# First and last rounds of an attention stage: values, adapter and feed-forward weights moved between rounds

## The chip, the cores and the metric

One Trainium2 chip, one of its cores. The metric is the device time of one execution of the whole program in microseconds (us), lower is better. Each kernel is run several times and the median counts.

## What is computed

The input is x of shape (4, 256, 512), that is four batches of 256 tokens with 512 channels. Three residual layers follow, with a feed-forward layer twice:

```python
x = x + attn_a(layernorm(x))     # causal attention, 32 heads of 16, rotary, plus an adapter of 10 tokens
x = x + ffn(layernorm(x))        # 512 -> 512, rows and columns chosen by 64 centroids
x = x + attn_b(layernorm(x))     # Mamba2 mixer: 128 heads of 64, 8 groups, state 128
x = x + ffn(layernorm(x))        # the same weights again

# attn_a
q, k, v = split(x @ w_attn.T); q, k = rope(q), rope(k)
y  = softmax(mask(q @ k.T / sqrt(16))) @ v
ak, av = adapter_wte @ w_attn.T
y += gating * softmax(q @ ak.T / sqrt(512)) @ av
out = y @ w_proj.T

# ffn
dots = softmax(x @ centroids.T / 0.1); hits = dots > 0.01
dense = x @ weight.T + bias
out = where(any(hits, 1)[:, None] & any(hits, 0)[assignments][None, :], dense, 0)
```

The column choice `any(hits, 0)` needs the hits of all 1024 tokens. So the first feed-forward layer can compute its dense part tile by tile, but it takes its results into x only when all eight tiles of 128 tokens are through.

## The kernel before

All of x lies in the on-chip memory as eight tiles of 128 tokens. A matrix product in 32-bit precision is made as three products of high and low parts (`mm3`, lines 107 to 114: L112 is high by high, L113 and L114 the two cross terms); `split` (L102 to L105) makes the parts, with a copy on ScalarE (ACT, L104) and a subtraction on VectorE (DVE) or on GpSimd (POOL) (L105).

`attention` (L232 on) works in 32 **rounds**: round i takes batch b = i // 8 and a step u = i % 8 of four heads. Round i computes the `scores` of its four heads on TensorE (PE, L441 and L448), their maxima on DVE (L453) and their exponentials on ACT (L456, eight activations, each with a read of the accumulator). Later rounds go on with it: round i + 1 turns the exponentials (`turn`, L471, PE transposes into the PSUM tile `ptr`, then copies, L472), round i + 2 weighs the values with them (`weigh`, L481 and L487), round i + 3 gathers the result into `y` (`gathered`, L498, L504).

Beside this main line, generators carry work that a round takes along. A generator yields a stage ("long", "values" or "turn") and the round from which it may go on; `step(stage, i)` moves those that are due. In before, `moved` treats round 0 as "the next round" (`v[1] if v[1] else i + 1`). The generators are:

- `prepared(b)`: norm of the batch's two token tiles (`normed`, transposes L163), queries, keys (`made`, 12 matmuls of 128x512 each, then the rotation on DVE L280 to L284 and POOL L286) and values (12 matmuls a tile, then an ACT copy, L383). For batch 0 it runs whole ahead of the rounds; for batches 1 to 3 it runs during the batch before.
- `pieces(b, q, f)`: builds the queries (f = 0) and keys (f = 1) of eight heads: `stacked` (ACT L304, POOL L305), then PE transposes into `trp` (L393) and copies L395, which are on DVE for f = 0 and on ACT for f = 1.
- `adapter`, `adapter_scores`, `adapted`: the ten adapter tokens.
- `closed(b, ks)`: the finished `y` is turned (L555) and projected (L566, 24 matmuls of 128x512 for a batch, tile `po`), then `finished` adds it to x (L582), and for batches 2 and 3 makes the statistics (L135, L136) and the root (L140, a square root on ACT, which needs another activation table than the exponential) of the feed-forward norm.
- `fed(f, t)`: one tile of the feed-forward layer: `normed` in the stage "turn", and `Feed.tile` in the stage "long" of the round after (24 matmuls of 128x288, tile `pd`, L112 to L114; then ten DVE instructions and one exponential, L205 to L218).

TensorE follows the order in which the program is written (`manual_schedule`). For the other engines and the DMA queue a planner fixes the order when the program is built: of what it takes to be ready it picks the earliest in program order.

The weights of the output projection (`wp`) are loaded and split ahead of the rounds, on ACT and POOL (`weights(wp_s, wproj, "pc1", nc.gpsimd)`, L629). The weights of the feed-forward layer (`fw`) are loaded and split when `Feed` is made, in round 24 (L679 to L689, L188 to L191), on ACT and DVE. Its eight tiles start ("turn") in the rounds `FEEDS = (25, 26, 27, 29, 31, 32)` and, for tiles 6 and 7, after the last projection; the 32nd and later "rounds" hold no scores any more and are called the tail here. After the tail `select` (L222) counts the hits and the mixer follows. It is the far longer part of the program.

The PSUM tiles are in rings: `m` with three buffers (`trp`, `ptr`, `pq`, `pd`, `po`, `tr` and others share them), `sc` with four for the scores, `py` with one.

Of the kernel before, what the change touches and what calls it, by code (L numbers as in the profile page):

```python
# [77 lines left out]
def hybrid_kernel(  # L78
# [93 lines left out]
    class Feed:  # L172


        def __init__(self, name, w1, p2):
# [12 lines left out]
            for k in range(KC):  # L188
                r = p2.tile([P, 2, FH], F32, name=f"{name}r", tag="fr")
                load(r, ffw[:, k])  # L190
                split([v[:, k] for v in self.w], r)  # L191
            self.new = t("x", [P, TT, C])
            self.hits = t("h", [P, NCL])
            nc.gpsimd.memset(self.hits, 0.0)

# [36 lines left out]
    def attention(later):  # L232
        with ExitStack() as es:
# [19 lines left out]
            def weights(w, src, tag, engine):  # L253
                for k in range(0, KC, 2):
                    r = p2.tile([P, 2, C], F32, name="ar", tag=tag)
                    load(r, src[:, k : k + 2, :])
                    for j in range(2):
                        split([v[:, k + j, :] for v in w], r[:, j, :], engine)
# [100 lines left out]
            def prepared(b):  # L359

                where = (ps, "m") if b else (ps_s, "sc")
                r = 8 * (b - 1)
# [17 lines left out]
                made(1, 1)  # L380
                for c in range(2):
                    yield "long", r + 5 + c
                    nc.scalar.copy(vs[b % 2][:, c, :C], projected(xs[c], wv_s, where))  # L383
# [160 lines left out]
            def closed(b, ks):  # L544
# [5 lines left out]
                yield "turn", 0  # L550
# [6 lines left out]
                if 3 not in ks:  # L557
                    return
                st = state.pop(b)
                pos = []  # L560
                for c in range(2):
                    if c == 0 or b < B - 1:
                        yield "long", 8 * b + {B - 1: 0, B - 2: 12}.get(b, 14) + c
                    pos.append(ps.tile([P, C], F32, name="po", tag="m"))
                    cs = slice(c * P, (c + 1) * P)
                    mm3(pos[c], [[v[:, k, cs] for v in st["yT"]] for k in range(KC)],  # L566
                        [[v[:, k, :] for v in wp_s] for k in range(KC)])
                    if b < B - 1:
                        finished(b, c, pos[c])
                if b < B - 1:  # L570
                    return
                for c, po in enumerate(pos):
                    finished(b, c, po)
                for t, xn in late.items():
                    tr = ps.tile([P, KC, P], F32, name="tr", tag="m")
                    xs = [p2.tile([P, KC, P], F32R, name=f"axs{j}", tag=f"axs{j}") for j in range(2)]
                    feed.norm.turn(xn, tr, xs)
                    late[t] = xs

            def finished(b, c, po):  # L580
# [4 lines left out]
                if feed is None:  # L585
                    return
                feed.norm.stats(t)
                feed.norm.root(t, t + 1)
                if b < B - 1:
                    slow.append(fed(feed, t))  # L590
                else:
                    late[t] = p2.tile([P, C], F32, name="axn", tag="t1")
                    feed.norm.scale(t, late[t])

            def fed(f, t):
                yield "turn", 0
                xs = normed(f.norm, t)
                yield "long", 0
# [25 lines left out]
            for _ in prepared(0):  # L624
                pass
            for t in range(2, TT):
                norm.stats(t)
            norm.root(2, TT)
            weights(wp_s, wproj, "pc1", nc.gpsimd)  # L629
            jobs, slow = [], []  # L630

            def adapter():
                split(wt, wte_s)
                yield "long", 0
                ak = adapter_weights()
                yield "turn", 0
# [8 lines left out]
            feed, late = None, {}  # L645
            asides, nexts = [], {}
            FEEDS = (25, 26, 27, 29, 31, 32)

            def moved(j, i):
# [4 lines left out]
                else:  # L654
                    nexts[j] = v[0], v[1] if v[1] else i + 1
# [5 lines left out]

            begin(0)
# [6 lines left out]
            with tc.manual_schedule(engines={nc.tensor.engine}):  # L669
                for i in range(n + 6):  # L670
                    b, u = divmod(i, 8)
                    if i < n:
                        if u == 0:
                            if i:
                                begin(b)
                            if b + 1 < B:
                                moved(prepared(b + 1), i)
                        es_[i] = scores(b, u)
                    if i == n - 8:  # L679
# [6 lines left out]
                        for t in range(4):  # L686
                            feed.norm.stats(t)
                        feed.norm.root(0, 4)
                        slow += [fed(feed, t) for t in range(4)]  # L689
                    if i in FEEDS:  # L690
                        moved(slow.pop(0), i - 1)
                    step("long", i)
                    if part:
                        next(part)
                    part = None
                    if i < n and u % 2 == 0 and i > 0:
                        asides.append(adapter_scores(b, u // 2))
                        next(asides[-1])
                    step("values", i)
                    if 2 <= i <= n + 1:  # L700
                        yss[i - 2] = weigh(*divmod(i - 2, 8), eTs.pop(i - 2))
                    if 1 <= i <= n:
                        eTs[i - 1] = turn(es_.pop(i - 1))
                    if 3 <= i < n + 3:
                        gathered(*divmod(i - 3, 8), yss.pop(i - 3))
                    while asides:
# [566 lines left out]
```

## Time and profile before

| what | value |
|---|---|
| median of 3 runs | 1900.88 us (1900.85 to 1903.54) |
| profiled execution, its own time | 1898.88 us |
| span of the profiled execution | 1897.1 us |
| mean granted TensorE clock | 0.988 |
| PE busy | 1813.4 us (96%) |
| DVE, ACT, POOL busy | 1474.0, 1381.5, 370.0 us |
| first scores of round 0 | 36.39 us |
| first scores of round 31 | 331.45 us |
| `select` after the first feed-forward layer (L222) | 376.60 us |

The span is the time from the first to the last instruction; the execution's own time has 1.8 us more around it, and lies 2.0 us under the median. "Busy" is the time in which an engine had an instruction running; a PE that is busy isn't one at its peak. A line of the timeline gives the start, the duration, the engine, the line of the kernel, the operation with its tiles (out<-in), the shapes and the number of merged instructions, and in brackets how long the engine had been idle before and what ended that. The view by stretches gives the busy time of each engine, the number of instructions in brackets, then the granted clock (1.00 is full), the share of DMA and GB/s.

### The profile page before, as it was taken

The numbers are of one execution on the slowest core, as the hardware profiler recorded it, in microseconds if no ns is written. First come the engines' busy times: TensorE is split into PE (matmuls) and PEld (weight loads), VectorE is DVE, ScalarE is ACT, GpSimd is POOL, SyncE is SP. The second block draws the span as 40 slices with busy tenths as digits, with TensorE's granted clock in tenths as the row PEclk, the third lists the DMA queues.
The fourth block names the chain that finished last, engine by engine and source line by source line (L and its number), as shares of the span: only waits on it lengthen the run. The fifth ranks groups of instructions, "written<-read, shape, count | busy, mean of one in ns | idle before, by whom it ended". The sixth has DMA issues, their size and how long they took to land.

```text
span 1897.1 us, 29902 instructions
## 1 busy us (share of the span) xinstructions
PE 1813.4 (96%) x10690; PEld 1450.5 (76%) x10690; DVE 1474.0 (78%) x2324; ACT 1381.5 (73%) x2875; POOL 370.0 (20%) x308
## 2 busy tenths in 40 slices
PE   7889989789999999999999999999999999999997
PEld 6667767676777887878788778777787888787786
DVE  6566667688998778777877787778778877877777
ACT  5667677368898768777877787678777876786753
POOL 5212110011311211211212121212221221122100
PEclk8999999999999999999999999999999999999999
DMA  4000000125555454554545464545554545455341
GB/s 142 1 1 1 22 15 1 32 62 172 176 188 180 147 170 150 160 157 150 170 150 158 145 184 144 176 143 167 149 171 143 158 156 164 148 162 166 112 124 49
DMA packets 151909, 240.35 MB, mean 127 GB/s; under 512 B 12368, under 2 KB 77520, under 8 KB 151760
## 3 DMA queue, kind: packets, MB, share of 16 engines
q1 hardware_dynamic: 151760, 238.44, 40.1%
q8 instruction: 84, 1.38, 0.3%
q14 instruction: 65, 0.53, 0.1%
HBM read 202.75 MB, written 35.65 MB: 126 GB/s over the span
## 4 chain that ended last, share of the span: by engine, by line
PE 75%; DVE 9%; ACT 9%; DMA 3%; issue 3%; POOL 1%; SPq 0%; DVEq 0%; ACTq 0%; POOLq 0%
PE pp L112 12%; PE pp L113 11%; PE pp L114 11%; PE pyy L991 8%; PE pog L112 6%; PE pog L114 6%; PE pog L113 6%; PE trx L976 3%; ACT e L456 3%; PE ptr L471 2%; DMA wor<-in_wout_dram 2%; DVE acc L917 1%; PE pd L114 1%; ACT L921 1%; DVE eT L472 1%
## 5 line engine op out<-in xcount | busy, mean ns | idle before, releaser
L112 PE MATMUL pp<-mx,w 128*128 128x512 f32 (+1 forms) x1160 | 465.5, 401 | 8.1 <-DVE acc L917 7.6
L114 PE MATMUL pp<-mx,w 128*128 128x512 f32 (+1 forms) x1160 | 454.3, 392 | 0.0
L113 PE MATMUL pp<-mx,w 128*128 128x512 f32 (+1 forms) x1160 | 454.2, 392 | 0.0
L917 DVE SCALAR_TENSOR_TENSOR acc<-pp,cw_s,acc 128x1012 f32<-128x1012 f32 (+2 forms) x240 | 304.9, 1270 | 23.0 <-ACT acc L910 22.4
L965 DVE TENSOR_TENSOR em<-em,gm 128x1536 f32<-128x1536 f32 x128 | 228.0, 1781 | 94.2 <-ACT em L959 85.9
L112 PEld LDWEIGHTS pp<-mx,w 128*128 128x128 f32 x1160 | 218.5, 188 | 65.7 <-issue 10.4
L953 POOL TENSOR_SCALAR_AFFINE_SELECT r<-r 128x512 f32<-128x512 f32 x128 | 153.0, 1196 | 526.7 <-DMA r<-cumd 433.8
L114 PEld LDWEIGHTS pp<-mx,w 128*128 128x128 f32 x1160 | 218.6, 188 | 45.3 <-issue 0.4
L113 PEld LDWEIGHTS pp<-mx,w 128*128 128x128 f32 x1160 | 218.8, 189 | 40.6 <-issue 0.7
L1014 POOL TENSOR_TENSOR sq<-sq,acc 128x1024 f32<-128x1024 f32 x55 | 132.7, 2412 | 574.3 <-ACT acc L1013 574.3
L104 ACT CAST w<-wr 128x512 fp32r<-128x512 f32 x144 | 88.4, 615 | 189.1 <-PE pp L113 158.3
L112 PE MATMUL pog<-wo,gh 128*128 128x512 f32 x512 | 204.6, 400 | 0.0
L114 PE MATMUL pog<-wo,gh 128*128 128x512 f32 x512 | 200.4, 392 | 0.0
L113 PE MATMUL pog<-wo,gh 128*128 128x512 f32 x512 | 200.0, 391 | 0.0
L958 ACT ACTIVATE em<-r,col_t 128x128 f32<-128x128 f32 x512 | 164.9, 390 | 48.2 <-PE pyy L991 46.5
L991 PE MATMUL pyy<-em,xd 128*64 128x256 f32 (+1 forms) x2048 | 189.1, 330 | 2.6 <-DVE em L965 2.6
L991 PEld LDWEIGHTS pyy<-em,xd 128*64 128x64 f32 x2048 | 134.1, 137 | 63.8 <-issue 21.7
L961 ACT ACTIVATE em<-r,col_t 128x128 f32<-128x128 f32 x512 | 166.5, 388 | 0.0
L949 DVE TENSOR_SCALAR em<-r,col_t 128x128 f32<-128x128 f32 x512 | 136.0, 325 | 12.2 <-PE pyy L991 10.1
L977 DVE TENSOR_TENSOR xd<-trx,dt_t 128x512 f32<-128x512 f32 x128 | 86.2, 683 | 56.1 <-PE trx L976 56.0
L105 DVE TENSOR_TENSOR w<-wr,w 128x512 fp32r<-128x512 f32 x139 | 98.3, 708 | 37.2 <-ACT w L104 36.8
L456 ACT ACTIVATE e<-sc,nmx 128x256 f32<-128x256 f32 (+1 forms) x256 | 103.4, 430 | 30.4 <-DVE nmx L453 30.4
(287 smaller groups left out, 3176.4 us busy)
## 6 DMA issues: line engine op xcount, KB each, us to landing
wr<-in_win_dram SPq DMA_DIRECT2D x287, 256.0 KB, 2.8
r<-cumd SPq DMA_DIRECT2D x128, 512.0 KB, 4.2
spill<-gb SPq DMA_DIRECT2D x63, 512.0 KB, 2.8
gr<-spill SPq DMA_DIRECT2D x120, 256.0 KB, 3.4
wor<-in_wout_dram SPq DMA_DIRECT2D x64, 256.0 KB, 3.1
out_dram<-x SPq DMA_DIRECT2D x8, 256.0 KB, 2.3
x<-in_x_dram SPq DMA_DIRECT2D x1, 1536.0 KB, 10.0
gr<-spill SPq DMA_DIRECT2D x8, 192.0 KB, 2.7
```

Source lines behind the costliest of these rows:

```text
L112: nc.tensor.matmul(o, lh, rh, start=(first and k == 0), stop=False)
L113: nc.tensor.matmul(o, lh, rl, start=False, stop=False)
L114: nc.tensor.matmul(o, ll, rh, start=False, stop=(last and k == n - 1))
L456: nc.scalar.activation(es_[c][:, 2 * j + pr, :], sc[:, j, :], AF.Exp, bias=nm[:, j : j + 1], accum_out=rs[:, c, h : h + 1],)
L917: nc.vector.scalar_tensor_tensor(av[:, :, d:], pv[:, :, : L - d], cw_s[:, ch, tap : tap + 1], av[:, :, d:], ALU.mult, ALU.add,)
L949: nc.vector.tensor_scalar(e[:, b, 2, :], rv[:, b, 1, :], col_t[:, h, b, 1:2], 0.0, ALU.subtract, ALU.min,)
L953: nc.gpsimd.affine_select(rv[:, :, 0, :], rv[:, :, 0, :], pattern=[[0, B], [1, P]], compare_op=ALU.is_ge, fill=-1e30, base=0, channel_mult ...
L958: nc.scalar.activation(e[:, b, 1, :], rv[:, b, 1, :], AF.Exp, bias=col_t[:, h, b, 2:3])
L961: nc.scalar.activation(e[:, b, 0, :], rv[:, b, 0, :], AF.Exp, bias=col_t[:, h, b, 0:1])
L965: nc.vector.tensor_tensor(e, e, gm, ALU.mult)
L991: nc.tensor.matmul(py[d, b, k * P :], xd[:, 2 * b + k, d], es2[hh][:, b, 2 * k : 2 if k == 0 else 3, :].rearrange("p s i -> p (s i)"), sta ...
L1014: (nc.gpsimd if n < NB - 1 else nc.vector).tensor_tensor(sq, sq, x2, ALU.add)
```

## The change

It reorders the attention stage; no arithmetic is changed.

1. **Values in the rounds.** `prepared(0)` no longer runs whole ahead of the rounds. Its norms, queries and keys do; its values (2 x 12 matmuls) come in the stage "long" of rounds 0 and 1, into PSUM ring `m` in place of `sc`. Round 0 is now a round of its own right, so `prepared(1)`, which had started in round 1, starts in round 0 and goes one round earlier throughout (norm in rounds 0 and 1, queries and keys in 1 to 4, values in 5 and 6).
2. **Projection weights.** `wp` is loaded in round 3, into a staging buffer that shares its place (`ya`) with the adapter's tokens and its products, and is split there.
3. **Feed-forward weights.** `Feed` is made at the end of round 23; a quarter of its weights is loaded and split at the end of each of the rounds 23 to 26, the subtraction on POOL in place of DVE. The statistics of the first four tiles go along, one a round, and their root follows at the end of round 26 (before: round 24).
4. **Feed-forward tiles.** Tiles 0 and 1 are turned in rounds 28 and 29 and multiplied in rounds 29 and 30; tile 2 is turned in round 31. Tiles 2 to 5 are multiplied in the tail, tiles 6 and 7 at its end as before. Before, tiles 0 to 3 were multiplied in rounds 26, 27, 28 and 30.
5. **Tail.** It is written out instead of running as rounds 32 to 37. Tile 4 is multiplied after the last `gathered`, the projection of batch 3 follows, and then tile 5, while the norms of tiles 6 and 7 are made.
6. **Roots.** Batch 2's two tiles share one root in place of one each.
7. The second feed-forward layer (`Feed("g")`) calls its weights in a loop of its own, on DVE as before.

```diff
-            for k in range(KC):
-                r = p2.tile([P, 2, FH], F32, name=f"{name}r", tag="fr")
-                load(r, ffw[:, k])
-                split([v[:, k] for v in self.w], r)
...
+        def weights(self, k, engine=nc.vector):
+            r = self.p2.tile([P, 2, FH], F32, name=f"{self.name}r", tag="fr")
+            load(r, ffw[:, k])
+            split([v[:, k] for v in self.w], r, engine)
...
-                r = 8 * (b - 1)
+                r = 8 * (b - 1) if b else -5
...
+                where = (ps, "m")
                 for c in range(2):
                     yield "long", r + 5 + c
                     nc.scalar.copy(vs[b % 2][:, c, :C], projected(xs[c], wv_s, where))
...
                 feed.norm.stats(t)
-                feed.norm.root(t, t + 1)
+                if b == B - 1 or c == 1:
+                    feed.norm.root(t if b == B - 1 else t - 1, t + 1)
...
-            weights(wp_s, wproj, "pc1", nc.gpsimd)
...
-            FEEDS = (25, 26, 27, 29, 31, 32)
+            FEEDS = {28: 0, 29: 1, 31: 2}
...
-                    nexts[j] = v[0], v[1] if v[1] else i + 1
+                    nexts[j] = v[0], i + 1 if v[1] is None else v[1]
...
+            first = prepared(0)
+            moved(first, -9)
+            while nexts[first][1] < 0:
+                moved(first, -9)
...
+                    if i in FEEDS:
+                        moved(fed(feed, FEEDS[i]), i - 1)
+                    if i == 3:
+                        weights(wp_s, wproj, "ya", nc.gpsimd, p1)
...
+                    if i in range(23, 27):
+                        feed.weights(i - 23, nc.gpsimd)
+                        feed.norm.stats(i - 23)
+                    if i == 26:
                         feed.norm.root(0, 4)
...
+                b = B - 1
+                step("long", n)
+                yss[n - 2] = weigh(b, 6, eTs.pop(n - 2))
+                eTs[n - 1] = turn(es_.pop(n - 1))
+                gathered(b, 5, yss.pop(n - 3))
+                step("turn", n)
+                moved(fed(feed, 3), n - 1)
+                step("turn", n)
+                step("long", n + 1)
+                step("values", n + 1)
+                yss[n - 1] = weigh(b, 7, eTs.pop(n - 1))
+                gathered(b, 6, yss.pop(n - 2))
+                moved(closed(b, (0, 1, 2)), n)
+                moved(fed(feed, 4), n)
+                step("turn", n + 1)
+                gathered(b, 7, yss.pop(n - 1))
+                moved(closed(b, (3,)), n)
+                step("long", n + 2)
+                moved(fed(feed, 5), n)
+                step("turn", n + 2)
+                pos = [projected_out(b, c) for c in range(2)]
+                late = {}
+                for c, po in enumerate(pos):
+                    t = 2 * b + c
+                    finished(b, c, po)
+                    late[t] = p2.tile([P, C], F32, name="axn", tag="t1")
+                    feed.norm.scale(t, late[t])
+                step("long", n + 3)
+                for t, xn in late.items():
+                    tr = ps.tile([P, KC, P], F32, name="tr", tag="m")
+                    xs = [p2.tile([P, KC, P], F32R, name=f"axs{j}", tag=f"axs{j}") for j in range(2)]
+                    feed.norm.turn(xn, tr, xs)
+                    late[t] = xs
+                for t, xs in late.items():
+                    feed.tile(t, xs, [ps_s.tile([P, FH], F32, name="pd", tag="sc") for _ in range(2)])
```

## Prediction

> **What bounds the kernel now.** I read the page first, then the chain of waits in order of time, then stretches cut at the first score matmul (L441) of each round, then PE's timeline. The change touches only the first 376.6 us; the mixer behind it keeps its instructions. The page's chain says what sets the pace over the whole span:
>
> ```profile
> PE 75%; DVE 9%; ACT 9%; DMA 3%; issue 3%; POOL 1%; SPq 0%; DVEq 0%; ACTq 0%; POOLq 0%
> ```
>
> That is an average, and ahead of round 0 it is wrong. There the chain runs through POOL:
>
> ```profile
> 25.71 1.25 POOL r L286
> ...
> 28.01 0.69 POOL wp L105
> ...
> 29.28 1.30 POOL wp L105
> 30.58 1.24 POOL r L286
> 31.82 1.92 POOL wp L105 x2
> ...
> 34.67 0.46 POOL st L305
> ...
> 36.39 1.12 PE sc L441 x8
> ```
>
> The last rotation (r, L286) and the last stack of keys (st, L305) queue behind the projection weights (wp), which nobody needs before round 14. In round 1, PE then waits for the adapter's keys:
>
> ```profile
> 49.56 1.03 PE L335 MATMUL tra<-con,st 20*128 20x20 f32 x8 [2.56 <-POOL st L305]
> ```
>
> Rounds 24 to 29 as stretches, and two pieces of the chain in rounds 24 and 25:
>
> ```profile
> 259.31:269.94 10.63, 7.72 (x66) 5.97 (x66) 8.79 (x20) 8.54 (x28) 3.85 (x5) 0.84 0.00 0
> 269.94:280.32 10.38, 7.59 (x71) 6.18 (x70) 4.07 (x9) 9.04 (x28) 0.87 (x2) 0.92 0.01 2
> 280.32:292.30 11.98, 10.98 (x91) 8.91 (x90) 10.06 (x28) 7.43 (x28) 0.92 (x2) 0.93 0.00 1
> 292.30:301.90 9.60, 8.96 (x81) 7.44 (x80) 6.98 (x19) 6.96 (x26) 1.08 (x2) 1.00 0.01 2
> 301.90:314.28 12.38, 11.65 (x94) 9.69 (x94) 10.29 (x27) 8.55 (x26) 0.00 (x0) 1.00 0.00 1
> 314.28:322.28 8.00, 7.84 (x67) 6.15 (x67) 5.29 (x12) 6.55 (x23) 0.00 (x0) 1.00 0.00 1
> ```
>
> ```profile
> 259.87 2.44 DVE fw L105 x2
> ...
> 272.09 1.28 ACT L456
> ```
>
> Rounds 24 and 25 have little for PE (7.7 and 7.6 us busy) and still take over 10 us. In 24, two feed-forward splits stand before the maxima on DVE; in 25 the exponentials wait for their table after the root. The tail lasts 45.15 us (331.45 to 376.60) with PE busy for 35.59; its worst place and its last two stretches:
>
> ```profile
> 339.59 0.40 PE L112 MATMUL pd<-fw,axs 128*128 128x288 f32 x1 [2.87 <-ACT axs L104]
> 340.72 0.44 PE L112 MATMUL pd<-fw,axs 128*128 128x288 f32 x1
> 356.38:366.82 10.44, 8.38 (x45) 6.07 (x41) 6.96 (x18) 3.93 (x8) 0.00 (x0) 1.00 0.00 0
> 366.82:376.60 9.78, 7.26 (x52) 6.87 (x52) 7.27 (x23) 4.87 (x10) 1.26 (x1) 1.00 0.01 2
> ```
>
> A tile multiplied right after its own turning makes PE wait 2.87 us, and the clock drops: its matmuls then follow each other at 0.24 us instead of 0.13.
>
> **Part by part, in us against the profiled span of 1897.1.**
>
> *First scores.* Without wp, the last rotation starts when DVE's L284 ends (28.63) and not at 30.58; the ACT copy (0.41) and the POOL part (0.46) follow at once, where st now waits from 32.3 to 34.67. So st ends at 31.0 instead of 35.13; transposes and copy (1.26 as now) bring the scores to 32.1: −4.3. The values leaving PE alone would bring little, as PE sat idle for 3.14 before the last trp. If DVE also puts the statistics of tiles 2 to 7 later, −5.2; if the planner fills POOL with something else, 0. I take −4.3, the reading of the chain itself.
>
> *Rounds 0 to 2.* Round 0 gets 12 value matmuls (12 x 0.233 = 2.8) and the transposes of a norm (0.6): +3.4, as it has only 0.67 of PE idle. Round 1 gets 12 values and the first 12 query matmuls of batch 1, 5.6; of these the wait of 2.56 and part of another 1.07 are cover: +2.2. Round 2 swaps queries for keys, loses a norm's transposes (0.6) and should start on a full clock (it ran half its time at the half clock, mean 0.88, because of round 1's idle): −2.0. Sum +3.6. Round 7 loses 12 matmuls and the wait on their copy (PE idle 1.69 before ptr, ended by ACT av L383): 8.95 falls to about 7.0, since a round with keys on ACT needs its exponentials, two copies and the turn, some 7 (round 3 takes 7.71): −1.9. So this part is +1.7; from +5.6 (nothing covered: 24 matmuls) to −2.1 (all 7.7 of PE idle in rounds 0, 1, 2 and 7 filled).
>
> *Projection weights in round 3.* Two loads on an idle DMA queue, four ACT copies (4 x 0.58), four POOL subtractions (4 x 1.28). Needed from round 14; ACT is busy 6.00 of 7.71 in round 3 and 5.45 of 9.60 in round 4. Behind POOL's four stand a rotation and stacks used a round later. If the shared buffer comes free only with batch 0's adapter products, the loads go to rounds 10 to 12 and still make round 14. Cost 0.4, from 0 to 2.3 (all four copies on the path).
>
> *Rounds 23 to 31.* Splits: one ACT copy (0.68) and one POOL subtraction a round, 1.28 x 576/512 = 1.44, where POOL is busy for 8.0 of 80.57. Round 24 then looks like round 16 (8.25, the same work without feed-forward): −2.4. Round 25 loses the table load and a tile's transposes: −2.3. Round 26 loses 24 pd matmuls (24 x 0.133 = 3.2) and transposes (0.6), and starts warm: −4.5. Round 27 loses the same 3.8 but receives the root with its two table loads (2 x 1.28 + 0.30), and exponentials and copies hold it at 7 anyway: −0.4. Round 28 loses 3.2 of pd, gains 0.6 of transposes: −2.8. Round 29 gains a tile, as PE is busy 7.84 of 8.00: +3.3. Rounds 30 and 31 keep theirs. Sum −9.1; from −5 (only the two stalls go) to −11. The merged root takes two loads (2 x 1.28) off ACT in round 28, but PE is idle there for only 0.7 and not because of them: 0.
>
> Here a page speaks for more. The Trainium skill, "ScalarE: Activation LUTs", section "What ACT_TABLE_LOAD costs", gives 2.66 us a switch with the drain, so the merged root would bring an estimated 5.3 and the forecast would fall by that. Another speaks against the change: "GPSIMD Engine Reference", section "Engine selection", says to keep elementwise work of two inputs on VectorE because GpSimd takes twice as long; were these four splits on the path, they would cost an estimated 3 instead of gaining. This case's rows decide both by who waits: nobody waits for POOL's fw, and DVE's 2.44 stand on the chain.
>
> *Tail.* Tiles 2 and 3 now stand where 4 and 5 stood, to 356.4, with the same waits. Then come tiles 4 and 5 as additions: 2 x (3.2 + 0.6) = 7.6. They cover a wait of 1.02 before the last try and most of one of 0.73 before tile 6; tile 4's own wait for its split costs about 0.7 and DVE's order about 0.3. DVE was busy some 15 of the last 20 and gets 2 x 4.0 (norm 0.55, split 0.69, ten small ones 2.8): 23 in 27. Tail +6.8; from +5.5 (waits filled) to +17.6 (below).
>
> *Sum:* −4.3 + 1.7 + 0.4 − 9.1 + 6.8 = −4.5. The span becomes 1892.6, the execution 1894.4 (1.8 more), and against the median 1900.9 − 4.5 = **1896.4 us**.
>
> **The rivals.**
>
> *A, slower: tiles 4 and 5 each pay the price of 339.59.* Place: after tile 4's transposes only one short gather stands before its matmuls. If ACT's copy queues behind the copies of yT, and DVE's part behind the adds of y, PE waits 2.87 and the clock drops, so that a tile costs 2.87 + 5.3 + 0.6 = 8.8: two are +17.6 where I have 6.8 after cover, net −4.3 + 1.7 + 0.4 − 9.1 + 17.6 = +6.3, or 1907.2. Against it: tile 5 has the 24 projection matmuls (5.6) between turn and use. It decides from about 1 us of wait before pd of both tiles.
>
> *B, no change: the first rounds give back what the preamble gains.* The scores come 4.3 earlier, but the 24 matmuls and the batch-1 work are covered by nothing: +5.6 in place of +1.7; and wp costs 1. Net about 0: −4.3 + 5.6 + 1.0 − 9.1 + 6.8 = 0.0, 1900.9. For it: PE idles longer ahead of round 0 and may start it cold (round 0 ran at 0.73 already).
>
> *C, the change does less than it says:* rounds 24 to 28 shorten only by their stalls (−5), because exponentials and the ring of three m buffers hold a round near 8: −0.4, 1900.5. Against it: round 21, with keys on ACT and 12 matmuls, takes 7.39.
>
> **How the numbers follow.** My case 0.60, A 0.17, B 0.12, C 0.11. A measurement of this kernel can tell about 0.2%, 3.8 us. Of my case some 0.50 lie beyond −3.8, 0.10 inside; A gives 0.16 slower and 0.01 same; B and C give 0.16 same, 0.03 faster, 0.04 slower. Together faster 0.53, same 0.27, slower 0.20. Low end: first scores −5.2, early rounds 0, rounds 23 to 31 −11, tail +5.5, wp 0, in sum −10.7: 1890. High end: A at 1907.
>
> **What would show it.** Right: first L441 near 32; no wp on POOL ahead of it; rounds 0 to 2 together near 35 (31.5 now); round 24 near 8.2 and round 26 near 7.5; no fw on DVE; first L441 of round 31 at 317 to 322; from there to L222 near 52. Wrong: a first L441 later than 34; rounds 24 to 28 in sum over 48 (55.0 now); PE waits over 2 us with the clock at 0.5 before pd of tiles 4 and 5; `select` after 377 by the trace's clock.

## The result, and the profile after

The changed kernel is slower by a third of a percent: 1907.19 us in the median of 7 runs (1905.57 to 1909.53) against 1900.85 us of 7 runs of the kernel before, a ratio of 1.0035, 95% interval 1.0023 to 1.0046. The forecast was 1896.4 us. The profiled execution took 1905.57 us, with a span of 1903.8 us (1.8 us lie around it, as before). In the traces the difference goes like this, in us against the kernel before (lengths are taken between the first score matmuls of the rounds; L441 is now L443, `select` is L223):

| stretch | predicted | trace of after |
|---|---|---|
| up to the first scores | −4.3 | −3.2 (36.39 to 33.20) |
| rounds 0 to 2 | +3.6 | +7.9 (31.5 to 39.4) |
| rounds 3 to 8, with wp | −1.5 | −0.65 |
| rounds 9 to 22 | 0 | −0.5 |
| rounds 23 to 30 | −9.1 | −10.1 |
| round 31 to `select` | +6.8 | +10.7 (45.15 to 55.82) |
| behind `select` | 0 | +2.5 |
| sum | −4.5 | +6.7 |

In rounds 9 to 22 the programs differ in one thing that the list of the change leaves out: the adapter's scores of the even rounds now come ahead of the stage "long". Every kernel below has this order too, and the −0.5 most likely comes from it (x8, otherwise as before up to round 22, has it as well, next to two halved clocks).

The page's chain hardly changed in its shares (PE 73% in place of 75%, ACT 12% in place of 9%), and tells nothing of this. The chain in order of time does, over the same stretch that was shown of before:

```profile
29.07 0.46 POOL st L306
29.53 1.23 POOL r L287
...
33.20 1.11 PE sc L443 x7
...
35.28 0.43 PE pq L112
...
39.45 0.23 PE pq L113
...
50.08 0.54 ACT wp L104
50.69 1.69 POOL wp L105 x2
...
53.17 1.27 POOL r L287
...
54.89 0.43 PE tra L336 x4
```

Three things are to be seen. No wp stands ahead of the last rotation any more (29.53, 30.58 before); a stack of the next pieces (29.07) has taken a little of its place. The values (pq L112 from 35.28) are now on the chain itself, at 0.43 us each, where the same kind of matmul takes 0.23 four us later. And wp is not in round 3: the planner found its loads and splits ready and drew them into rounds 0 and 1, where they and the rotation of batch 1 (53.17) stand ahead of the adapter's keys, which PE waits for at 54.89 (49.56 before).

PE's timeline shows where the clock went, with the idle time in brackets:

```profile
27.18 0.87 PE L395 MATMUL trp<-con,st 128*128 128x128 f32 x8 [1.78 <-POOL st L306]
31.77 0.75 PE L395 MATMUL trp<-con,st 128*128 128x128 f32 x4 [3.73 <-POOL st L306]
```

With the values ahead of round 0 and no wp (x3 below), PE has one wait of 1.50 us in this place. The stretches (rounds 0, 1 and 2; then round 24; then round 31 to `select`; start and end, length, busy time of PE, PE's weight loads, DVE, ACT and POOL, then PE's clock):

```profile
33.20:44.04 10.84, 10.71 (x49) 8.06 (x49) 4.50 (x11) 7.19 (x24) 2.31 (x4) 0.72 0.15 49
44.04:58.46 14.42, 11.89 (x78) 9.61 (x78) 6.31 (x13) 9.73 (x34) 8.37 (x11) 0.92 0.13 37
58.46:72.60 14.14, 13.59 (x85) 10.35 (x84) 7.62 (x14) 6.32 (x24) 2.23 (x4) 0.84 0.00 0
...
263.05:273.17 10.12, 7.59 (x65) 6.06 (x64) 8.12 (x18) 9.52 (x29) 4.08 (x5) 0.83 0.00 0
...
324.92:380.74 55.82, 44.85 (x318) 38.24 (x317) 35.39 (x102) 23.28 (x58) 3.94 (x5) 0.94 0.06 19
```

Round 0 is full of PE (10.71 of 10.84) at a clock of 0.72. Round 26 is as short as hoped (7.83 us), with rounds 25, 27 and 28 (7.70, 6.25 and 9.57 us); round 24 is not, and the end is 4 us longer than expected. On the chain, round 24 waits for the root of tiles 0 to 3 and its two table loads, which the program has at the end of round 26:

```profile
264.78 1.28 ACT L140
266.08 0.30 ACT frs L140
266.39 1.28 ACT L458
```

Places of PE and ScalarE's activation tables in the end (332.95 is tile 2, 352.67 tile 4, 370.11 the turning of tile 7, 371.59 tile 6):

```profile
332.95 0.61 PE L112 MATMUL pd<-fw,axs 128*128 128x288 f32 x1 [2.81 <-ACT axs L104]
...
352.67 0.40 PE L112 MATMUL pd<-fw,axs 128*128 128x288 f32 x1 [0.51 <-ACT axs L104]
...
370.11 0.97 PE L163 MATMUL tr<-con,axn 128*128 128x128 f32 x4 [3.14 <-DVE axn L155]
...
371.59 0.44 PE L112 MATMUL pd<-fw,axs 128*128 128x288 f32 x1
```

```profile
358.00 1.28 ACT L140 ACT_TABLE_LOAD   x1
...
365.96 1.28 ACT L209 ACT_TABLE_LOAD   x1 [3.41 <-DVE fnm L207]
...
367.68 1.28 ACT L140 ACT_TABLE_LOAD   x1
```

The exponential of tile 5 was set between the roots of tiles 6 and 7, so ACT changes its table twice more, the scaling of tile 7 comes late, PE idles 3.14 us and multiplies tile 6 at half the clock. Tiles 4 and 5 themselves waited 0.51 us and not at all.

### The profile page after: what moved, and what is told of

Same layout as the page of the kernel before. It is cut to its first block, busy times and chain, and to the rows that moved or that the text cites. A ratio compares the mean times of both kernels' runs of the same rounds, so it can differ in the third digit from the quotient of the medians.

```text
span 1903.8 us, 29900 instructions
## 1 busy us (share of the span) xinstructions
PE 1815.8 (95%) x10690; PEld 1453.8 (76%) x10690; DVE 1473.3 (77%) x2319; ACT 1379.9 (72%) x2874; POOL 346.9 (18%) x312
## 4 chain that ended last, share of the span: by engine, by line
PE 73%; ACT 12%; DVE 8%; DMA 3%; issue 3%; POOL 1%; SPq 0%; ACTq 0%; DVEq 0%; POOLq 0%
PE pp L112 12%; PE pp L113 11%; PE pp L114 11%; PE pyy L1016 8%; PE pog L112 6%; PE pog L114 6%; PE pog L113 6%; ACT e L458 4%; PE trx L1001 3%; DMA wor<-in_wout_dram 1%; PE ptr L473 1%; DVE acc L942 1%; ACT L946 1%; PE pg L956 1%; ACT acc L946 1%
## 5 line engine op out<-in xcount | busy, mean ns | idle before, releaser
L112 PE MATMUL pp<-mx,w 128*128 128x512 f32 (+1 forms) x1160 | 465.1, 401 | 9.1 <-DVE acc L942 8.6
L112 PEld LDWEIGHTS pp<-mx,w 128*128 128x128 f32 x1160 | 218.2, 188 | 66.9 <-issue 11.0
L978 POOL TENSOR_SCALAR_AFFINE_SELECT r<-r 128x512 f32<-128x512 f32 x128 | 125.1, 977 | 548.9 <-DMA r<-cumd 484.6
L112 PE MATMUL pog<-wo,gh 128*128 128x512 f32 x512 | 204.4, 399 | 0.0
L974 DVE TENSOR_SCALAR em<-r,col_t 128x128 f32<-128x128 f32 x512 | 137.7, 328 | 12.6 <-PE pyy L1016 10.1
```

The source lines that it names most:

```text
L112: nc.tensor.matmul(o, lh, rh, start=(first and k == 0), stop=False)
L974: nc.vector.tensor_scalar(e[:, b, 2, :], rv[:, b, 1, :], col_t[:, h, b, 1:2], 0.0, ALU.subtract, ALU.min,)
L978: nc.gpsimd.affine_select(rv[:, :, 0, :], rv[:, :, 0, :], pattern=[[0, B], [1, P]], compare_op=ALU.is_ge, fill=-1e30, base=0, channel_mult ...
```

## Experiments

Theory: the loss is made in the first rounds (values without cover, on a halved clock) and at the end (the tables' order), while the rounds between do what they should. Rivals: wp's new place, the earlier start of batch 1, or the late part as a whole is the cause. Every kernel x1 to x14 was timed together with the kernel before (13 to 34 runs of it each time, medians 1901.5 to 1902.6). The third column is the start of round 9, the fourth of `select`, both from one trace each. Kernels that differ from each other only behind round 22 (x5, x7, x9, x10, x11) lie up to 3.0 us apart at round 9, so a single trace tells less than the ratios do. Ratios of kernels that were timed together (x1 to x4, x5 to x8, x9 to x12, x13 and x14) compare best.

| kernel | ratio (95%) | round 9 | `select` |
|---|---|---|---|
| before | 1 | 118.63 | 376.60 |
| after | 1.0035 (1.0023 to 1.0046) | 122.72 | 380.74 |
| x1 root first | 1.0014 (1.0006 to 1.0023) | 122.32 | 379.05 |
| x2 first part undone | 0.9994 (0.9985 to 1.0003) | 119.75 | 378.02 |
| x3 values back | 0.9983 (0.9974 to 0.9993) | 114.68 | 375.65 |
| x4 wp back | 1.0030 (1.0017 to 1.0044) | 125.86 | 383.54 |
| x5 x3, batch 1 later | 0.9988 (0.9977 to 0.9999) | 118.69 | 376.84 |
| x6 fillers | 1.0003 (0.9990 to 1.0016) | 120.35 | 377.89 |
| x7 four edits | 0.9968 (0.9956 to 0.9980) | 116.83 | 375.71 |
| x8 late part alone | 0.9996 (0.9986 to 1.0006) | 119.08 | 379.86 |
| x9 x7, root late | 0.9986 (0.9974 to 0.9998) | 115.73 | 376.58 |
| x10 x7, tile 2 earlier | 0.9961 (0.9945 to 0.9976) | 118.38 | 370.44 |
| x11 x7, both | 0.9971 (0.9959 to 0.9983) | 116.33 | 374.68 |
| x12 x11, batch 1 early | 0.9957 (0.9945 to 0.9970) | 114.19 | 370.16 |
| x13 x10, batch 1 early | 0.9947 (0.9934 to 0.9959) | 114.53 | 368.23 |
| x14 values stay, three costs out | 0.9972 (0.9961 to 0.9983) | 119.35 | 372.68 |

### Values and projection weights, one at a time

x3 puts the values back, x4 wp, x2 both (the first two edits together):

```diff
 x3:
-            first = prepared(0)
-            moved(first, -9)
-            while nexts[first][1] < 0:
-                moved(first, -9)
+            for _ in prepared(0):
+                pass
...
-                where = (ps, "m")
 x4:
-                    if i == 3:
-                        weights(wp_s, wproj, "ya", nc.gpsimd, p1)
...
+            weights(wp_s, wproj, "pc1", nc.gpsimd)
             begin(0)
```

> The kernel after with its first rounds as in the kernel before: values of batch 0, statistics of the other tiles and the load of wp all ahead of round 0. Rounds 23 and later and the end stay as after. Theory (the first part costs 4.1 us, all of it seen at the start of round 9): round 9 starts near 118.6 us instead of 122.7, the gains of rounds 24 to 30 (about -10) and the dear end (+10.7) stay, and the time is about 1903.1. Rival (what is late at round 9 is hidden later, or the gains of rounds 24 to 30 came only from being late): round 9 near 118.6 but the selection still near 380, time about 1907.

> The kernel after with only batch 0's values put back ahead of round 0 (wp stays in round 3 by the program, where the planner is free to move its loads and splits forward). Theory A (the idle TensorE before round 0 and its halved clock during the value products are most of the +4.1): TensorE shows no halved clock from 29 to 39 us, first scores near 33 to 34 plus nothing, round 0 near 6 and round 1 near 11, round 9 near 119.5, time about 1904. Theory B (the splits of wp on GpSimd and ScalarE ahead of batch 1's rotation and the adapter's keys are the cost): round 9 stays at 121.5 to 122.7, time about 1906 to 1907.

> The kernel after with only the load and split of wp put back ahead of round 0, as in the kernel before; the values of batch 0 stay in rounds 0 and 1. Theory A (cold clock and values are the cost): round 9 moves by less than 1.5 us, to 121.3 to 122.7, time about 1906. Theory B (wp's splits in rounds 0 and 1 are the cost): round 9 near 119, time about 1903.5.

With after itself this is a table of two by two. Moving the values into the rounds costs 6.1 us at round 9 with wp ahead (x2 to x4) and 8.0 us with wp later (x3 to after); in the ratios 0.0036 and 0.0052, that is 7 and 10 us. Counted from the first scores, rounds 0 to 8 take 82.2 us (x2), 81.9 (x3), 89.9 (x4) and 89.5 (after): 7.7 us for the values in both pairs, 0.4 for wp.

Moving wp gains 5.1 and 3.1 us at round 9, nearly all of it ahead of the first scores. In time, x3 is 2.4 us faster than x2, which was timed with it (medians 1897.88 of 12 runs and 1900.32 of 11); between x4 and after (+0.0005) nothing can be told.

So the values are the loss, as theory A of x3 has it, and more strongly than expected (1897.9 us where 1904 was written); x3 alone turns the change into a gain. That a halved clock is most of their price, as the theory also says, these runs do not show (x6 below), and x3 has one itself, from 33.8 to 37.2 us. x2 is faster than its theory too (1900.3 us for 1903.1), with round 9 a little later than named, and x4's round 9 came 3.1 us later, where theory A had named less than 1.5.

The values bring nothing in return at the first scores that can be told: 32.83 us with them ahead (x3), 33.20 without (after). Traces of kernels that are the same up to there differ by more: 33.20 and 34.81 (after, x1), 35.34 to 37.55 (before, x2, x8).

### The halved clock

```diff
+            dummy = ps_y.tile([P, L], F32, name="warm", tag="py")
+            fill += [lambda: None, lambda: warmed(dummy, [ones] * 6), lambda: None,
+                     lambda: warmed(dummy, [ones] * 14)]
+            with tc.manual_schedule(engines={nc.tensor.engine}):
                 for f in range(2):
                     for _ in pieces(0, 0, f):
                         pass
```

> The kernel after with 6 and 14 throw-away 128x128 products of a constant set into TensorE's two idle places ahead of round 0 (1.78 and 3.73 us); the values stay in rounds 0 and 1. They feed nothing. Theory (of the +8.0 us that the two value tiles cost, 24 products by 0.233 us = 5.6 us are plain uncovered TensorE time and the rest, about 2.3 us, is the halved clock from 29 to 39 us): TensorE's clock stays full into round 0, rounds 0 and 1 together 23 us instead of 25.3, time about 1905. Rival A (the clock is all of it, the products are hidden): rounds 0 and 1 together near 17.5, time near 1899. Rival B (the clock costs nothing, the rounds wait for ScalarE): rounds 0 and 1 stay at 25, time 1907.

The fillers in PE's timeline, and the stretch of round 0 (values still in it):

```profile
28.12 3.36 PE L119 MATMUL warm<-ones 128*128 128x128 f32 x28
```

```profile
32.45:40.59 8.14, 8.01 (x49) 6.01 (x50) 3.48 (x8) 6.89 (x23) 2.31 (x4) 1.00 0.23 65
```

The fillers keep the clock at 1.00, the values follow each other at 0.23 us (33.97 and 34.20), and round 0 takes 8.14 instead of 10.84 us (8.13 in x14, which has the fillers too); rounds 0 and 1 together are 22.5 us (23 was written, 25.3 in after, 17.4 in x3). So of the values' price 5.1 us stay at the full clock, close to 24 x 0.233 = 5.6, and 2.7 us were the clock. The time fell by more than that, from 1.0035 to 1.0003 (1902.1 us, where about 1905 was expected). Of the 4.8 us between the two traces 2.4 lie ahead of round 9 and 2.0 behind `select`, where the instructions are the same.

### The end

x1 changes one order on ScalarE:

```diff
-                step("long", n + 3)
+                with tc.issue_after(rooted):      # rooted: the root of tile 7
+                    step("long", n + 3)
```

> The kernel after, with one order added: on ScalarE the exponential of feed-forward tile 5 is queued behind the root of tile 7. Theory (the +10.7 us between the first scores of round 31 and the selection's first matmul is in part ScalarE's order root 6, exponential 5, root 7, exponential 6, with four table loads, which makes the transposes of tile 7 wait 3.14 us): one Sqrt load and one Exp load are left in the tail, tile 7's transposes start some 3 to 4.5 us sooner, the stretch goes from 55.8 to about 51.3 us, the selection from 380.7 to about 376.2, and the time from 1907.2 to about 1902.7. Rival (the products of tiles 4 and 5 on the path are the whole cost, the tables lie beside them): the stretch stays at 55 to 56 us and the time at 1907.

```profile
369.59 0.66 PE L163 MATMUL tr<-con,axn 128*128 128x128 f32 x4 [0.77 <-DVE axn L155]
```

The wait of 3.14 us is 0.77, one load each way is left, and the stretch falls from 55.82 to 53.22 us: 2.6, where 4.5 had been expected. That this is about 2 x 1.28 us, the two loads that went, is chance, for the order itself gave 3.5 us: from the first transpose of tile 6 to `select` after, x2, x4, x5, x6 and x8 take 14.33 to 14.40 us, and every kernel with x1's order 10.82 to 10.85. x1's trace lost 0.9 of it earlier in the stretch, where tile 2 ran at half the clock for 6.83 us and not for 3.41. x3, whose trace has the old order and the same wait of 3.14 but no halved clock behind it, takes 12.85; so of the 3.5 us some 2 are the wait and 1.5 the halved clock that followed it.

The time fell by 0.0021, to 1905.06 us where 1902.7 had been expected. The planner had then set the exponential of `a_s` between two roots of the mixer, which gave a pair of loads back at 382.37, and the stretch behind `select` is the longest of the sixteen traces (1524.5 us); the later kernels with this order queue the mixer's first root behind that exponential.

x10 turns tile 2 a round earlier, on top of x7 (below):

```diff
-            FEEDS = {28: 0, 29: 1, 31: 2}
+            FEEDS = {28: 0, 29: 1, 30: 2}
```

> The four edits together, plus tile 2 of the feed-forward layer turned in round 30 instead of 31, so that its products stand in round 31 behind the scores instead of right behind its own turning at the head of the tail. Theory (the wait of 2.81 us before pd of tile 2 and the halved clock behind it are a price that a tile pays when multiplied right after its turning; elsewhere it costs 3.8): from the first scores of round 31 to the selection 53.5 becomes 49 to 50, round 30 grows by 0 to 1 for the transposes, time about 1893.5. Rival (TensorE is full there and the wait moves to the turn of round 31's exponentials): 53 stays, time 1897.

```profile
322.63 0.38 PE L112 MATMUL pd<-fw,axs 128*128 128x288 f32 x1
...
323.43 0.29 PE L112 MATMUL pd<-fw,axs 128*128 128x288 f32 x1
323.56 0.30 PE L113 MATMUL pd<-fw,axs 128*128 128x288 f32 x1
```

Tile 2 waits for nothing and runs at 0.13 us a matmul (0.24 at 332.95 of after). Round 31 to `select` takes 48.78 instead of 53.49 us, round 30 grows by 1.0, and `select` comes at 370.44 instead of 375.71. Theory confirmed in the trace, with a part that is chance: of the 5.3 us, 1.6 is a longer halved clock in rounds 24 and 25 of x7's trace, and tile 2 ran at half the clock for 6.83 us in x7, where it did for 3.41 in after (6.26 against 5.01 us for its matmuls). In time it is 0.9968 to 0.9961, within the intervals.

### The late part alone, and the root of round 24

x8 is the kernel before up to round 22 but for the place of the adapter's scores, with rounds 23 on as after: the edits of x2, which leave batch 1 starting in round 0, and

```diff
-                r = 8 * (b - 1) if b else -5
+                r = 8 * (b - 1) + (b == 1) if b else -5
```

> The kernel before with only the late part of the change: everything up to round 22 as before (values and wp ahead of round 0, batch 1's preparation from round 1), rounds 23 and later and the end as after. Theory (rounds 24 to 30 give 10.3 us and the end takes 10.7): the start of round 9 near 118.6, the selection within 1 us of the kernel before's 376.6, time 1900.5 to 1902. Rival (the prediction's sum, -9.1 + 6.8): the selection near 374.3, time about 1898.7.

0.9996, 1901.2 us: what rounds 24 to 30 give, the end takes. The trace's `select`, at 379.86, is 3.3 us behind that of before; 3.2 of it are halved clocks in rounds 9 and 17 (13.08 and 13.02 us, 11.47 and 11.46 in before), which have nothing to do with the late part. The forecast's −2.3 lies inside the interval as well (−2.7 to +1.1 us).

> The four edits together (0.9968 of the time of the kernel before), plus one order: the root of feed-forward tiles 0 to 3 is queued on ScalarE behind the last exponential of round 26, where the program writes it; the planner had drawn it into round 24. Theory (the prediction's term for round 24, -2.4, came out at -0.5 to +0.3 because the root's two table loads still stand ahead of that round's exponentials, and the idle time then halves the clock): round 24 falls from 10.97 to about 8.4 us and round 25 from 8.40 to 7.7, round 27 pays at most 1, and the first scores of round 31 come 2 to 3 us sooner, time about 1894.5 to 1895. Rival (the switch costs its 2.7 us in round 27 as well): first scores of round 31 within 0.7 us of 322.2, time 1897.

```diff
-                        feed.norm.root(0, 4)
+                        with tc.issue_after(last_exp[0].ins):   # of round 26
+                            feed.norm.root(0, 4)
```

The stretches of rounds 24 and 27 of x7:

```profile
258.81:269.78 10.97, 8.44 (x65) 6.31 (x64) 8.12 (x18) 9.78 (x29) 4.08 (x5) 0.76 0.00 0
...
286.00:292.26 6.26, 5.08 (x53) 3.71 (x52) 4.23 (x9) 5.31 (x23) 0.17 (x1) 1.00 0.00 0
```

Rounds 24, 27 and 28 of x9:

```profile
257.65:265.92 8.27, 6.51 (x66) 4.94 (x66) 7.32 (x16) 7.21 (x27) 4.40 (x6) 1.00 0.00 0
...
282.57:290.50 7.93, 5.33 (x55) 3.80 (x54) 4.19 (x9) 7.50 (x25) 0.88 (x2) 0.93 0.00 0
290.50:302.63 12.13, 11.17 (x73) 8.82 (x73) 7.03 (x16) 5.87 (x24) 0.87 (x2) 0.76 0.01 1
```

Rounds 24 and 25 do as the theory says (8.27 and 7.69, from 10.97 and 8.40), and rounds 26, 27 and 28 give all of it back and 2 us more: +1.1 (7.82 to 8.96), +1.7 and +2.6 (9.57 to 12.13). ScalarE is the longest engine of round 27 (7.50 of 7.93), and the chain runs through the root and both loads (279.87 and 284.73) there too; PE then idles 2.25 us before `try` at 289.88, and round 28 starts at half the clock (0.76). The rival is right, and the ratio got worse (0.9986).

### Batch 1's start, and the parts together

> The kernel after with batch 0's values put back ahead of round 0 (1897.9 us as measured alone) and, on top, batch 1's preparation one round later (first turn in round 1, values in rounds 6 and 7, as the kernel before had it). The diff moves it one round earlier, which no step of the prediction priced. Theory (the early start costs: round 0 carries a normalisation and tile turn, 6.93 against 6.05 us; rounds 8 and 9 lack the cover of the value tile, 9.22 and 13.03 against 8.26 and 11.47): round 0 near 6.1, round 7 near 8.9, rounds 8 and 9 together near 20, round 10 starts near 125.5 instead of 127.7, time about 1895.7. Rival (the tile only changes place): 1897 to 1898.

The theory falls: 0.9988 against 0.9983 without the edit (x3). (The forecast did price the early start, in its rounds 0 to 2 and 7.) Round 0 is shorter (6.14 against 6.93), but round 1 is longer by 1.5, and a halved clock came into round 7. The other pairs lean the same way: batch 1 in round 0 is faster by 0.0014 (x12 against x11), 0.0014 (x13 against x10) and 0.0002 (x2 against x8). Only x12 and x11 were timed together, with medians of 1893.80 and 1896.65 us (11 and 10 runs), and the traces of the first three pairs start round 10 some 2.1 to 2.4 us earlier. So the early start is no cost, and more likely a gain of 1 to 3 us, though no pair's intervals lie apart.

x7 is x5 with the order of x1 and the mixer's first root behind `a_s`; x11 adds the edits of x9 and x10, x12 takes back that of x5, x13 takes back that of x9 as well. x14 is after with the fillers of x6, both orders of the end and x10's edit.

> The kernel after with four edits: values of batch 0 ahead of round 0, batch 1's preparation one round later, on ScalarE the exponential of tile 5 behind the root of tile 7, and the mixer's first root behind the exponential of a_s (in the run with the root first alone, the planner had put that exponential between two roots of the mixer, two more table loads). wp and rounds 23 and later as after. Theory: the sum of the parts, 1895.7 for the first two, 2 to 2.6 us off the end: about 1893.3. Rival (the mixer takes the end's gain back): 1895.5 or more.

> The four edits, the late root and the earlier tile 2 in one kernel. If the theories of the two single runs hold and the parts add up: the selection 6 us sooner than with the four edits alone (375.7), near 370, time about 1891.5. If both are rivals' cases: 1897.

> The same without the edit on batch 1: its preparation starts in round 0 as in the kernel after. If the early start costs nothing that can be measured (0.9983 against 0.9988 in the pair of runs without the other edits): within 2 us of the run with all edits. If it helps by as much as that pair's traces say (2.4 us at the start of round 10): 2 us faster. If it costs, as was first thought: 2 us slower.

> The kernel after with batch 0's values ahead of round 0, batch 1's preparation left in round 0 as after has it, the exponential of tile 5 behind the root of tile 7, the mixer's first root behind a_s, and tile 2 turned in round 30. The root of tiles 0 to 3 is left to the planner. Expected from the run with batch 1 later (0.9961) and from the pair with the late root (0.9957 against 0.9971): 0.9950 to 0.9961, that is 1893 us beside a kernel before at 1902; the selection near 369 to 370. If the gain of the pair was chance: 0.9961.

> The kernel after with its values left in rounds 0 and 1 as the change has them, and the three costs that were found taken out together: filler products ahead of round 0 (they feed nothing), the order of the roots with the mixer's first root behind a_s, and tile 2 turned in round 30. Theory (the three costs and the values' 24 uncovered products of 0.233 us are the whole miss): the selection near 370.5 to 371 (377.9 with the fillers alone, less 2.3 and 4.7), ratio 0.9965 to 0.9975, about 1896, and slower than the run with the values ahead of round 0 by about 5.6 us less what that run loses to its own cold clock, so by 1 to 5 us. Rival (another cost of the values remains): the selection over 373, ratio 0.999 or more.

x7 came out at 0.9968: below x5, timed with it, by 2.4 us in the medians and 3.8 in the ratios, where 2 to 2.6 were expected of the end; 1897.3 us in place of 1893.3, since x5 had not brought what it was credited with. x11 misses its sum, as x9 is a loss. x13 beats both kernels: 0.9947, some 8 to 10 us below before, with `select` at 368.23. x14 tests the account as a whole: with the values left in the rounds, but without the three costs, the kernel is at 0.9972, as the theory said (0.9965 to 0.9975), and above x13 by 0.0025 in the ratios (4.8 us) and by 2.5 us in the medians of 9 and 5 runs. Its trace lies between the two cases (`select` at 372.68; 371 and 373 had been named).

## Why the prediction was wrong

Between the forecast (−4.5) and the trace (+6.7) lie 11.2 us, and 8.2 of them are two steps of the sum: rounds 0 to 2 (4.3) and the tail (3.9). Of the forecast's own signs of being wrong one came, `select` at 380.74, later than 377; the other three did not.

*Rounds 0 to 2, +3.6 against +7.9: the first step that failed.* The 24 matmuls and the norm's transposes were counted rightly for round 0 (+3.4; at a full clock x6 takes 8.14 and x7, without the transposes of a norm, 4.55). But they were priced at the full clock. Taking the values out of the preamble left PE idle for 1.78 and 3.73 us there, and its clock was halved from 29.0 to 39.2 us: 2.7 us (x6). The forecast named this under rival B and put no price on it. In round 1, waits were to cover 3.4 of 5.6 us, but PE's idle time there only fell from 4.2 to 2.5 us: wp, which the planner drew forward, and batch 1's rotation took POOL ahead of the adapter's keys, and the round grew by 3.5 instead of 2.2 (x4, with wp out of the way, takes 13.56 in place of 14.42). Round 2 was to start at the full clock for −2.0; it started at half of it again (56.3 to 63.1 us) and gave −0.4. Its clock of 0.88 in before had also been read as half the round at the half clock; it is a quarter (3.41 of 14.55 us). Rival B's mechanism is what happened, at a higher price than its +5.6: with round 7, which gave −1.0, these rounds came to +6.9.

*First scores, −4.3 against −3.2.* The forecast's own terms give 32.3 (31.0 and 1.26), so −4.1. The mechanism is confirmed, its size only roughly: wp alone gives −4.7 from x2 to x3, but traces scatter here by up to 2.2 us, and with the values ahead the mean is 36.4 with wp ahead (before, x2, x8) and 33.7 with wp later (x3, x5, x7, x9 to x13), so −2.7. In after's trace two stacks on POOL (28.29 and 29.07) come ahead of the last rotation, which starts at 29.53 where 28.63 was forecast; the forecast had named this as what could fill the gap. The last transposes then run at half the clock (0.75 against 0.53 us). "The values leaving PE alone would bring little" agrees with the runs (−1.6 from x2 to x4, +0.4 from x3 to after, both inside the scatter). What it missed is that the reverse isn't true: where they lay they cost nothing that can be told, and in rounds 0 and 1 nearly their full length (5.1 of 5.6 us at the full clock).

*Projection weights in round 3, 0.4.* Wrong place: an edit that is written in round 3 is done when its inputs are ready, here in rounds 0 and 1. Moving it out of the preamble gains 2.4 us in time with the values ahead (x2 to x3) and nothing that can be told with the values in the rounds (x4 to after).

*Round 7, −1.9 against −1.0, and round 8, +0.95.* A round that loses PE work shows waits of its own: in round 7 PE now waited 1.66 and 1.58 us before `ptr` (110.46 and 112.70), for copies of DVE and ACT, where it had waited once for 1.69; and the clock was halved at 114.3, in round 8.

*Rounds 23 to 31, −9.1 against −10.1.* The sum held, by errors of its parts that cancel. Round 24 gave −0.5 instead of −2.4, as the root with its loads was drawn into it, and round 27, freed of the root, −3.35 instead of −0.4; round 26 gave −4.15 (7.83 us) of −4.5, round 29 grew by 4.1 for 3.3. x8 shows that the whole late part, with the tail, is worth about nothing.

*Tail, +6.8 against +10.7: the second step that failed.* Rival A put the price at tiles 4 and 5, and its time, 1907.2 us, is met by chance: these tiles hardly waited (0.51 us and nothing). The forecast's count of ten DVE instructions a tile was right and its ACT instruction was left out: one exponential, which the planner set between two roots. In the traces that costs 3.5 us, the two table loads, the wait and the halved clock behind it together (x1 and the kernels with its order). The remaining 7.1 stand against 6.8.

The pages of the Trainium skill that the forecast weighed come out so. The four splits on POOL took 1.42 us each in after, against 0.75 for most of those on DVE in before, but nobody waited for them, and the slower engine cost nothing. The twofold time that "GPSIMD Engine Reference", section "Engine selection", gives for elementwise work of two inputs is about what these rows show. On the chain of round 24 a root with a table load on either side took 2.91 us (264.78 to 267.69). The Trainium skill, "ScalarE: Activation LUTs", section "Table sets: the hidden batching unit", puts an exponential followed by a square root at about 5.3 us; the measurement is well below that, and decides. No run takes the merged root of batch 2 back by itself, so the forecast's 0 for it is not tested.

*Behind `select`, 2.5 us.* Each engine's order of instructions is the same there in before and after, and the stretch took 1519.4 to 1524.5 us in the sixteen traces. After's has a halved clock at 1472.8 us, the only one between 400 and 1880 us in any of them, and with PE's instructions matched one by one against before, 2.4 of the 2.5 us arise between 1466 and 1479 us. So in this trace it is that one fall. The medians differ by about as much as the traces do (6.3 and 6.7 us); whether the other runs lost time there too stays open.

## What to carry to other kernels

Work that fills a wait has no price where it lies; before it is moved, ask what else keeps the engine busy there, and price the place it goes to at the clock it will find. An instruction's place in the program is not its time: where a planner orders the engines, each moved load, root and exponential must be asked what it can be drawn ahead of or put between, and the one that matters be tied to a neighbour (x1). A saving in one round counts only when the rounds behind it have room for it: x9 gave its gain back within four rounds, and in x8 the end took what the rounds before had gained.

## What was not expected of the hardware

PE's clock is halved without any long wait. In seven of these traces it fell in round 9 or 17 (in x8 in both), which the others passed at full speed with the same work (about 11.5 us, and about 13.0 with the fall, so each fall costs 1.6 us). The 3.41 us ahead of such a fall in x7 (at 124.6), as a stretch like those above:

```profile
121.23:124.64 3.41, 2.22 (x20) 2.03 (x18) 1.06 (x3) 3.13 (x11) 2.10 (x3) 1.00 0.03 5
```

PE was 65% busy, and no single wait there was over 1.2 us. The halved stretches last 3.41 us or a multiple (up to 13.65), and within each trace they start whole multiples of 3.413 us apart, so the clock changes on a fixed grid.

Where this grid lies against the kernel differs from one execution to the next, and that goes with the falls. Round 9 has one in the four traces in which a point of the grid lies 7.5 to 8.0 us behind its first scores, and in none of the other twelve; round 17 in the four in which one lies 7.2 to 7.9 us behind. So a difference of some 1.6 us between two single traces can be nothing but this, and so can a part of the readings above.

The Trainium skill, "TensorE: Matmul & The Clock Gate", section "HAM oscillation — how this bites in real kernels", gives as a rule that PE should have no idle gap over about 3.4 us. These traces say that it is not enough: a halved clock also came behind 3.41 us in which no wait was over 1.2 us. How busy PE must be isn't shown: a fall came behind 79% of busy time (x1 at 59.4), and none behind 45% (after at 380.5).
